# Which engine weighs which gathered rows in the attention layer of a two-layer graph network

## The chip, the cores and the metric

The kernel runs on one core of a Trainium2 chip. The core has five engines that matter here, each with its own queue of instructions that it works through strictly in order: PE (TensorE, matrix products), DVE (VectorE), ACT (ScalarE), POOL (GpSimd, which here does hardly anything but issue the gathers) and SP (SyncE, which issues the plain transfers). They meet only through semaphores. The metric is the time of one execution on the device in microseconds (us), lower is better, given as the median of several executions.

## The reference

Two graph layers work on 1250 nodes of 512 features and 40000 edges, of which each has a source and a destination. The first layer is an attention (8 heads of 64 channels) followed by a feed-forward network (FFN), the second adds edge features, sums over edges and runs two dense layers with batch norms. The change lies in the attention, where each edge's row `xl[src]` is weighted and the weighted rows of a destination are summed:

```python
xl = (x @ Wl).reshape(-1, HEADS, C)
xr = (x @ Wr).reshape(-1, HEADS, C)
h = jax.nn.leaky_relu(xl[src] + xr[dst], NEG_SLOPE)
e = jnp.einsum('ehc,hc->eh', h, att)
m = jax.ops.segment_max(e, dst, num_segments=N_NODES)
ex = jnp.exp(e - m[dst])
denom = jax.ops.segment_sum(ex, dst, num_segments=N_NODES)
alpha = ex / (denom[dst] + 1e-16)
msg = alpha[..., None] * xl[src]
out = jax.ops.segment_sum(msg, dst, num_segments=N_NODES)
```

After it come a residual sum, a layer norm and `gelu(h @ W1 + b1) @ W2 + b2`, and then the second layer.

## The kernel before

**Stages.** The profiled execution has four stretches. Up to some 99 us the kernel sorts the nodes by their number of edges, projects the nodes and writes the table `xl_t` to memory. From there to some 880 us runs the attention with its FFN mixed in. Then comes the second layer's sum over edges (to some 1330 us) and its dense end.

**Blocks, groups, chunks.** The nodes are put in ten blocks of 128, one node for each partition, by number of edges. A block of `KB[b]` edge slots (25 to 44) is cut into groups of at most 20 slots, and a group into chunks of four or five (`parts(n, CN)`; the very first chunk has two). There are 22 groups and 77 chunks, 28 chunks of five rows and 48 of four. A *row* is one slot of the chunk: 128 partitions by 512 values (8 heads by 64, with one more column for each head). A chunk's rows are gathered by POOL, one indirect transfer for each row, into a buffer `xg`, of which there are seven (`GB`).

**One step of the main loop** (in `attention`) takes chunk c of the present group and one chunk of the group before:

1. `scores(g, c)`: POOL's gathers for the chunk are queued; DVE does a max, a min, a product with signs (all into `z`) and a reduction into `S`. At a group's last chunk `softmax` follows on DVE.
2. Small pieces of other work are queued: parts of the FFN and of the norms of finished blocks.
3. `weigh` of one chunk of the group before. DVE multiplies the last rows of the chunk with their weights `w` in a single product (`V.tensor_mul`). ACT weighs the first `na` rows, each as eight instructions (one for each head, 128 partitions by 64 values, with the weight as scale). After each ACT row one part of the FFN is queued (`some(1)`), and after the rows what is left of the step's quota of three or four parts. A part is four products `pu` on PE, a GELU `uT` on ACT and a product into `py` on PE. Only then come PE's products that add the chunk's rows up (`add_up`, tile `sums`), taken from the two ends of the chunk in turn: the last row, the first, the last but one, the second and so on. The last row is always DVE's and the first always ACT's.
4. At a group's last chunk `exp(g)` is queued on ACT and gives the weights `w` of the present group.

When a group's sums are complete, `leave()` copies them with ACT (`ab`), folds them with PE (`pacc`), and `merge` adds them with DVE (`acc`). Finished blocks go through `head_of` (transposes on PE, `aT` and `hT` and a square root `rs` on ACT, sums and statistics on DVE) and then through the FFN.

**What sets the order.** `V`, `A`, `T` and `G` are wrapped so that each engine runs in the order of the program. A buffer `xg` is free for a new gather once PE has summed its rows; with seven buffers and groups of four chunks the sums of a step free the buffer of the chunk that DVE scores three steps later.

**The line that is changed** sets `na` in `weigh`. Before, it gives ACT one row of each chunk in the last group; elsewhere it gives two rows of four, and two and three rows of five in turn (two where `c` is even, three where it is odd). ACT has 166 of the 333 rows in all.

Of the kernel before, what the change touches and what calls it, by code (L numbers as in the profile page):

```python
# [725 lines left out]
def gnn_kernel(ctx, tc, x, src, dst, edge_attr, ln1_g, ln1_b, Wl, Wr, att, gat_bias,  # L726
# [519 lines left out]
    def attention(s1, xb_t, xo_t, eb_t, back, lone, follow):  # L1246
# [281 lines left out]
        def some(n):  # L1528
            for _ in range(min(n, quota[0])):
                quota[0] -= 1  # L1530
                part()
# [43 lines left out]
        def row_of(g, j):  # L1575
            c = [i for i, (c0, cn) in enumerate(g["cuts"]) if c0 <= j < c0 + cn][0]
            return g["xg"][c][:, j - g["cuts"][c][0], :].rearrange("p (h c) -> p h c", c=CX)[:, :, 1:]

        def add_up(g, j, i):

            row = row_of(g, j)
            for k in range(2):
                r = slice(k * H2, k * H2 + H2)
                T.matmul(heads(g["sums"][k][i * H2:i * H2 + H2, :]), ident[r, r], row[r], start=not g["at"][i],
                         stop=g["at"][i] == g["rows"][i] - 1)
            g["at"][i] += 1

        def weigh(g):

            w, n = g["w"], g["n"]  # L1590
            g["gd"] = gd = sp.tile([P, HEADS], F32, name="gd")
            V.tensor_reduce(gd, w[:, :n, :].rearrange("p n h -> p h n"), axis=AX.X, op=OP.add)
            g["at"], g["rows"] = [0, 0], [sum((cn + 1 - i) // 2 for _, cn in g["cuts"]) for i in range(2)]
            for c, (c0, cn) in enumerate(g["cuts"]):
                na = 1 if g is groups[-1] else (cn + c % 2) // 2
                rest = leave()
                xv = g["xg"][c][:, na:cn, :].rearrange("p n (h c) -> p n h c", c=CX)[:, :, :, 1:]
                V.tensor_mul(xv, xv, w[:, c0 + na:c0 + cn, :, None].to_broadcast([P, cn - na, HEADS, CH]))
                for j in range(c0, c0 + na):
                    xv = row_of(g, j)  # L1600
                    for h in range(HEADS):
                        A.activation(xv[:, h, :], xv[:, h, :], AF.Copy, scale=w[:, j, h:h + 1])
                    some(1)
                    next(rest, 0)
                some(quota[0])
                for _ in rest:
                    pass
                if not c:
                    g["sums"] = [aq.tile([P, D], F32, name=f"sums{k}") for k in range(2)]
                for j in range(cn):  # L1610
                    add_up(g, c0 + j // 2 if j % 2 else c0 + cn - 1 - j // 2, j % 2)
                yield
            weighed.append(g)

        def leave():

            if weighed:
                g = weighed.pop()
                g["pacc"] = pacc = aq.tile([P, D], F32, name="pacc")
                for k in range(2):  # L1620
                    ab = bp.tile([P, D], F32, name="ab")
                    A.copy(ab, g["sums"][k])
                    yield
                    T.matmul(pacc[k * H2:k * H2 + H2, :], fold, ab, start=True, stop=True)
                folded.append(g)
# [50 lines left out]
        groups, weighed, folded = [], [], []  # L1676
# [8 lines left out]
        for i, g in enumerate(groups):  # L1685
# [14 lines left out]
            for c in range(nc_):  # L1700
# [4 lines left out]
                if c == 0:  # L1705
                    if not i:
                        others.append(wr_order())
                    if g["first"] and g["b"] != ORDER[-1]:
                        others.append(slots_of(g["b"] - 1))
                    if g is groups[-1] and held["xx"] < 3:  # L1710
                        rows_of(blk)
                    weighing = weigh(groups[i - 1]) if i else None
# [24 lines left out]
        for _ in weigh(g):  # L1737
            if folded:
                merge(folded.pop())
# [278 lines left out]
```

## Time and profile before

| what | value |
|---|---|
| median of 9 runs | 1482.49 us (1477.83 to 1486.03) |
| the profiled execution's own time | 1483.55 us |
| its span in the profile | 1481.8 us |
| granted TensorE clock | 0.912 |

Busy time of each engine in the four stretches, in us:

| stretch | PE | DVE | ACT | POOL |
|---|---|---|---|---|
| 0 to 150 | 91.8 | 116.9 | 68.1 | 74.9 |
| 150 to 880 | 592.0 | 605.8 | 507.5 | 464.2 |
| 880 to 1330 | 376.5 | 357.1 | 85.1 | 313.2 |
| 1330 to 1482 | 113.9 | 65.1 | 54.6 | 13.8 |

How to read what follows. The groups of instructions give out<-in by the program's tile names, the shapes, a count, then after the bar the busy time in us and the mean duration of one in ns, then the engine's idle time just before them and what ended it. The waits give who waited for whom, the total in us, how many times, and the longest. The timeline gives the start in us, a duration in us, the engine, the line, the instruction and a count of equal ones that were merged; in square brackets stands the engine's idle time before it and what ended that. All instructions of the attention carry the line of one helper, L782, so they are told apart by their tiles. ACT's small instructions overlap: eight of them are 2.02 us from first start to last end, though each lasts some 345 ns.

### The profile page before, as it was taken

Reading aid. Unit: us, or ns where it says so; the run is one execution under the profiler, and the core shown is the slowest. Engines: PE = TensorE matmul, PEld = TensorE weight load, DVE = VectorE, ACT = ScalarE, POOL = GpSimd, SP = SyncE. Lnnn points to the kernel's source line nnn. Section 1 sums busy time; section 2 is a strip of 40 time slices with the busy share of each in tenths; the row PEclk is TensorE's granted clock in tenths of the full one; section 3 lists DMA queues with packets and bytes.
Section 4 is the critical chain, followed back from the end, with each engine's and each line's share of the span. In section 5 each row is a group of like instructions: output and inputs, shape, how many; then the busy total and the mean of one; then the engine's idle time right before and its main releaser. Section 6 shows DMA issues by size and latency. Waiting matters only on the chain. (4 is left out here: it accounts for less than half of the span.)

```text
span 1481.8 us, 16505 instructions
## 1 busy us (share of the span) xinstructions
PE 1174.3 (79%) x5204; PEld 559.8 (38%) x5204; DVE 1144.9 (77%) x1472; ACT 715.3 (48%) x2063; POOL 866.0 (58%) x789
## 2 busy tenths in 40 slices
PE   6845659898988795978797797787787999898893
PEld 4431115344534442424353363222222443334452
DVE  7859898978888979898899512798988889877133
ACT  4525476867777676777856841111111222212533
POOL 2357777755577877674774003777777777750002
PEclk9977779999999798989898998999989999999996
DMA  6246966655566657553563043877777777760001
GB/s 223 93 144 175 397 181 180 181 146 154 147 186 181 191 174 195 167 160 109 159 177 94 19 153 112 292 238 245 229 233 235 231 239 242 224 180 22 0 0 72
DMA packets 89152, 251.16 MB, mean 170 GB/s; under 512 B 17214, under 2 KB 19268, under 8 KB 88543
## 3 DMA queue, kind: packets, MB, share of 16 engines
q0 software_dynamic: 61008, 199.11, 46.0%
q1 hardware_dynamic: 28047, 50.91, 9.6%
q8 instruction: 43, 0.70, 0.2%
q14 instruction: 54, 0.44, 0.1%
HBM read 225.86 MB, written 24.22 MB: 169 GB/s over the span
## 5 line engine op out<-in xcount | busy, mean ns | idle before, releaser
L782 POOL DMA_INDIRECT xg<-xl_t,src_i x333 | 422.2, 1268 | 197.8 <-issue 117.1
L749 POOL DMA_INDIRECT xs<-xb_t,src_i x333 | 314.9, 946 | 113.2 <-issue 59.4
L782 ACT ACTIVATE xg<-xg,w 128x64 f32<-128x64 f32 x1328 | 331.0, 344 | 0.1
L782 PE MATMUL sums<-xg,ident 64*64 64x512 f32 x1332 | 212.6, 715 | 112.4 <-DVE xg L782 105.0
L1826 PE MATMUL pe<-we,eaT 64*128 64x512 f32 x666 | 206.8, 683 | 71.5 <-DVE xs L1871 67.1
L782 DVE TENSOR_TENSOR z<-xg,nxr 128x1440 f32<-128x1440 f32 (+4 forms) x154 | 197.7, 1325 | 41.9 <-DMA xg<-xl_t,src_i 41.4
L782 DVE TENSOR_REDUCE S<-z 128x32 f32<-128x2080 f32 (+2 forms) x77 | 192.2, 2496 | 2.6
L782 PEld LDWEIGHTS pu<-hT,w 128*128 128x128 f32 x1280 | 165.9, 198 | 68.7 <-issue 58.1
L1871 DVE TENSOR_TENSOR xs<-xs,pe 128x1024 f32<-128x1024 f32 (+1 forms) x130 | 153.6, 1187 | 35.2 <-DMA xs<-xb_t,src_i 29.3
L782 PE MATMUL pu<-hT,w 128*128 128x128 f32 x1280 | 174.4, 285 | 0.0
L782 PE MATMUL py<-w,uT 128*128 128x512 f32 x320 | 163.4, 602 | 12.5 <-ACT uT L782 12.3
L1872 DVE SCALAR_TENSOR_TENSOR pd<-xs,pd 128x1024 f32<-128x1024 f32 (+1 forms) x130 | 155.7, 1198 | 3.3
L782 PEld LDWEIGHTS sums<-xg,ident 64*64 64x64 f32 x1332 | 60.0, 154 | 253.5 <-DVE xg L782 126.0
L1826 PEld LDWEIGHTS pe<-we,eaT 64*128 64x128 f32 x666 | 60.0, 198 | 169.9 <-DVE xs L1871 123.0
L1868 ACT ACTIVATE xs<-pe 128x1024 f32<-128x1024 f32 x40 | 41.0, 1024 | 160.0 <-PE pe L1867 136.6
L782 DVE TENSOR_TENSOR xg<-xg,w 128x1024 f32<-128x1024 f32 (+2 forms) x77 | 100.1, 1305 | 0.0
L782 ACT ACT_TABLE_LOAD x71 | 91.1, 1283 | 7.3 <-DVE sh L782 4.3
L782 PE MATMUL pacc<-ab,fold 128*64 128x512 f32 x88 | 55.0, 711 | 42.9 <-ACT ab L782 41.6
L741 POOL DMA_INDIRECT out_dram<-z,v_i x10 | 10.0, 1002 | 130.5 <-ACT z L782 128.0
L1867 PE MATMUL pe<-xs,ident 128*128 128x512 f32 x160 | 83.0, 628 | 2.0 <-DMA xs<-xb_t,src_i 1.9
L782 DVE TENSOR_TENSOR z<-z,sgn 128x768 f32<-128x768 f32 (+2 forms) x77 | 78.2, 1015 | 0.0
L782 PE MATMUL pz<-z,v 128*128 128x512 f32 (+1 forms) x192 | 71.0, 529 | 6.2 <-ACT z L782 6.2
(264 smaller groups left out, 1286.7 us busy)
## 6 DMA issues: line engine op xcount, KB each, us to landing
eb_t<-fe SPq DMA_DIRECT2D x38, 256.0 KB
ea<-eb_t SPq DMA_DIRECT2D x38, 256.0 KB
w<-in_L_gnn_W_dram SPq DMA_DIRECT2D x8, 1024.0 KB
xg<-xl_t,src_i POOLq DMA_INDIRECT x333, 3.9
xs<-xb_t,src_i POOLq DMA_INDIRECT x333, 3.8
v<-in_L_gnn_W_dram SPq DMA_DIRECT2D x2, 2048.0 KB
xo_t<-xo SPq DMA_DIRECT2D x10, 256.0 KB
x_out<-xo_t SPq DMA_DIRECT2D x10, 256.0 KB
```

What stands on the lines that cost most here:

```text
L741: s = nc.gpsimd.indirect_dma_start(out=table, out_offset=bass.IndirectOffsetOnAxis(ap=idx, axis=0), in_=rows, in_offset=None, bounds_check ...
L749: return nc.gpsimd.indirect_dma_start(out=rows, out_offset=None, in_=table, in_offset=bass.IndirectOffsetOnAxis(ap=idx, axis=0))
L782: ins = getattr(engine, name)(*args, **kw)
L1826: nc.tensor.matmul(pe[:, k, :], eaTs[n][r, j // 2, :], we[r, :], start=True, stop=not by_pe(i))
L1867: nc.tensor.matmul(pe[:, k, :], ident, xs[:, k, :], start=False, stop=True)
L1868: nc.scalar.activation(xv, pe, AF.Relu)
L1871: add = nc.vector.tensor_add(xv, xv, pe[:, :m, :])
L1872: nc.vector.scalar_tensor_tensor(pv, xv, 0.0, pv, op0=OP.max, op1=OP.add)
```

## The change

In every group but the last, ACT now has three rows of every chunk of five, and of chunks of four two rows (where `c` is even) and three (where it is odd). DVE has the rest.

```diff
             for c, (c0, cn) in enumerate(g["cuts"]):
-                na = 1 if g is groups[-1] else (cn + c % 2) // 2
+                na = 1 if g is groups[-1] else (cn + 1 + c % 2) // 2
                 rest = leave()
                 xv = g["xg"][c][:, na:cn, :].rearrange("p n (h c) -> p n h c", c=CX)[:, :, :, 1:]
                 V.tensor_mul(xv, xv, w[:, c0 + na:c0 + cn, :, None].to_broadcast([P, cn - na, HEADS, CH]))
                 for j in range(c0, c0 + na):
                     xv = row_of(g, j)
                     for h in range(HEADS):
                         A.activation(xv[:, h, :], xv[:, h, :], AF.Copy, scale=w[:, j, h:h + 1])
                     some(1)
                     next(rest, 0)
                 some(quota[0])
```

By the cuts of the groups this moves one row from DVE to ACT in 31 of the 77 chunks: in the 12 chunks of five with an even `c`, and in the 19 chunks of four with an odd `c`. ACT's rows go from 166 to 197. In the built program DVE's product goes from 24 by 64 values in each partition to 16 by 64 in the first kind, from 16 by 64 to 8 by 64 in the second, and ACT gets eight instructions more for each. The third row's FFN part, queued by `some(1)`, comes out of the same quota, so PE's and POOL's instructions are the same in number.

## The prediction

> **What bounds the kernel now.** First the windows, cut at the stages: the change touches 99 to 850 us only. In the row for 150 to 880 us the columns are the stretch, its length, the busy time of PE, PE's weight loads, DVE, ACT and POOL, then clock, DMA share and GB/s.
>
> ```profile
> 150.00:880.00 730.00, 591.98 (x3109) 292.57 (x3110) 605.84 (x687) 507.54 (x1683) 464.19 (x370) 0.91 0.57 168
> 250.00:300.00 50.00, 42.71 (x232) 19.33 (x228) 49.25 (x53) 39.63 (x129) 35.90 (x29) 0.94 0.65 181
> ```
>
> DVE is busiest (83%), PE close behind (81%), ACT has 70%. No engine is the bound alone: three queues wait on each other in turn. So I read next, in the same stage, the groups with shapes kept apart and the waits:
>
> ```profile
> L782 ACT ACTIVATE xg<-xg,w 128x64 f32<-128x64 f32 x1247 | 311.3, 345 | 0.1
> L782 DVE TENSOR_TENSOR xg<-xg,w 128x1024 f32<-128x1024 f32 x60 | 72.5, 1214 | 0.0
> L782 DVE TENSOR_TENSOR xg<-xg,w 128x1536 f32<-128x1536 f32 x13 | 22.7, 1749 | 0.0
> DVE z L782 <- DMA xg<-xl_t,src_i: 32.0, 13, 5.9
> DVE gd L782 <- ACT w L782: 12.5, 4, 7.0
> PE sums L782 <- DVE xg L782: 82.6, 21, 6.8
> PE sums L782 <- ACT xg L782: 3.2, 5, 0.8
> ACT hT L782 <- PE pt L782: 46.3, 10, 7.1
> ```
>
> The sums wait for DVE far oftener than for ACT, which speaks for moving rows away from DVE. But DVE's own longest single wait on ACT is 7.0 us, for the weights `w`, and ACT's idle time (730 - 507.5 = 222 us) is not spread evenly: it lies in waits for PE's transposes and projections. What counts is therefore where each added row falls: in front of such a wait, or inside a run in which ACT never rests.
>
> **The change, part by part.** *Removed from DVE:* 31 rows. Three rows cost 1749 ns, two 1214, so a row is 0.535 us; for a product cut from two rows to one I take the same step (the one-row product of the first chunk lasts 0.68 us, again 0.53 less). 31 x 0.535 = 16.6 us of DVE time. *Added to ACT:* 31 x 8 instructions. In the timeline 16 of them take 3.93 us and 8 take 2.02, so eight more are 1.91 us; 31 x 1.91 = 59 us. ACT would go to (507.5 + 59) / 730 = 78%, DVE to 81%. *Moved:* the third row's FFN part. It stays ahead of the sums in PE's queue, but its GELU sits behind one more ACT row. That is 1.9 us, and the part's product into `py` comes three parts (over 5 us of PE work) later, so I cost it at nothing; without that cover it would cost PE up to 1.9 us a step. The gathers are not moved, but a buffer comes free later where the sums end later. The new row also comes before its neighbour in the sums of chunks of four (last, first, third, second), so two rows (0.9 us) follow ACT's end instead of one.
>
> Behind the added row wait, on ACT's queue: the next GELUs, the copies `ab`, the weights `w`, the root `rs`. For `w` and `rs` DVE waits, for `ab` PE. I lined up the 77 chunks from the timeline (end of DVE's product, end of ACT's rows, the sums) and followed a delay through each stretch that has affected chunks, until an idle gap takes it up:
>
> 1. *99 to 250 us: -2.1.* DVE hardly rests, ACT waits for it. Four of six affected chunks give their 0.535 us. The other two (183 to 200 us) give nothing: there the sums already end on ACT's rows.
> 2. *250 to 306 us: +1.2.* Four affected chunks, and ACT is busy 39.6 of 50 us. Two rows from 254 on push `w`, `ab` and `acc` until a 2.1 us gap at 267 takes half; the sums at 277 move by 2.0, the rows before 284 by 1.6 + 1.9, and `hT` at 288.3 by 1.2, after PE's own idle time before the sums (1.6 us) is eaten. DVE waits for this chain at 300.5 (5.2 us), so its 4 x 0.535 is lost.
> 3. *306 to 366 us: +0.8.* The row added at 323 ends after DVE's product and holds the sums by 0.8; the other two cancel (+0.3 and -0.4).
> 4. *366 to 432 us: 0.* Three affected chunks, in front of ACT waits of 0.9 to 4.7 us; DVE's gain becomes more waiting for gathers (4.3 us at 420).
> 5. *432 to 470 us: +1.9.* ACT's rows end at 441.7 and the sums at 442.8. One more row (with 0.9 us of sums behind it instead of 0.5) moves the sums, then PE's projection, the next sums, and with them the buffer that POOL waits for at 456; DVE waits for just that gather. (The stretch's second affected chunk stands before 6 us of ACT idleness.)
>
> ```profile
> 439.65 2.01 ACT L782 ACTIVATE xg<-xg,w 128x64 f32<-128x64 f32 x8
> 440.87 1.95 PE L782 MATMUL sums<-xg,ident 64*64 64x512 f32 x16
> 455.14 1.95 PE L782 MATMUL sums<-xg,ident 64*64 64x512 f32 x16
> 457.89 2.29 POOL L782 DMA_INDIRECT xg<-xl_t,src_i  x1 [1.80 <-ACT xg L782]
> 469.55 2.94 DVE L782 TENSOR_TENSOR z<-xg,nxr 128x1800 f32<-128x1800 f32 x2 [5.09 <-DMA xg<-xl_t,src_i]
> ```
>
> 6. *470 to 500 us: -1.1.* Two affected chunks with PE waiting for DVE (5.0 and 5.5 us).
> 7. *500 to 706 us: 0.* Three affected chunks, each before 1.4 to 4.7 us of ACT idleness and with the sums 5 us after ACT.
> 8. *706 to 756 us: +1.1.* ACT runs without a gap from 705.8 to 737.8 and gets three rows, +5.7. The gap of 4.8 before `hT` (742.6) takes most; `hT` comes at 737.8 + 5.7 = 743.5 or just after, some 1.1 later, and with it `rs`, for which DVE already waits 2.1 us.
> 9. *756 to 814 us: -1.6.* DVE never waits; three rows less.
> 10. *814 to 841 us: +3.8.* ACT's run from `hT` to `w` has no gap, two of its four chunks get a row, and DVE waits for `w`:
>
> ```profile
> 814.43 1.51 ACT L782 ACTIVATE hT<-pt,cols 128x128 f32<-128x128 f32 x4 [6.52 <-PE pt L782]
> 824.40 3.93 ACT L782 ACTIVATE xg<-xg,w 128x64 f32<-128x64 f32 x16
> 833.50 3.93 ACT L782 ACTIVATE xg<-xg,w 128x64 f32<-128x64 f32 x16
> 837.45 1.28 ACT L782 ACT_TABLE_LOAD   x1
> 838.74 0.26 ACT L782 ACTIVATE w<-S 128x72 f32<-128x72 f32 x1
> 839.04 0.27 DVE L782 TENSOR_REDUCE gd<-w 128x8 f32<-128x64 f32 x1 [7.01 <-ACT w L782]
> ```
>
> After it comes the tail of the attention, which the second layer waits for: DVE's product, the sums, the fold, the last block's FFN. None of it has slack, so +3.8 goes to the end.
>
> Sum of the ten: -2.1 + 1.2 + 0.8 + 1.9 - 1.1 + 1.1 - 1.6 + 3.8 = +4.0 us. The profiled execution took 1483.55 us (its span 1481.8 and 1.75 around it), so 1487.5; it is 1.1 above the median of the nine runs, and from that median I forecast 1482.5 + 4.0 = 1486.5.
>
> What the trace of before cannot show is how the queues settle after several shifts. From below: every chunk whose sums start 0.1 us after DVE's product gives its 0.535 and no wait on ACT grows. I count 14, so -7.5. From above: every affected chunk whose sums end 3 us or less after ACT's rows (ten) passes on the whole row: 10 x 1.91 = +19. I take +4.0, nearer to the first, since most rows fall before gaps.
>
> *A rule against the change.* In the rows a moved row costs ACT 1.91 us and spares DVE 0.535. The Trainium skill, "ScalarE: Activation LUTs", section "Rules for kernel authors", says that multiplications belong on VectorE and not on ScalarE. By that rule alone the sum would be 59 - 16.6, some 42 us slower; the waits above say that most of it lies in ACT's gaps, and the waits decide here.
>
> *A rule on the gathers.* In the trace a gather's issue takes 0.95 us beside DVE's reductions, and more beside its products of two tensors:
>
> ```profile
> 506.17 2.94 DVE L782 TENSOR_TENSOR z<-xg,nxr 128x1800 f32<-128x1800 f32 x2 [1.99 <-DMA xg<-xl_t,src_i]
> 506.55 2.47 POOL L782 DMA_INDIRECT xg<-xl_t,src_i  x1 [0.30 <-issue]
> 510.21 2.86 DVE L782 TENSOR_REDUCE S<-z 128x40 f32<-128x2600 f32 x1
> 511.30 0.95 POOL L782 DMA_INDIRECT xg<-xl_t,src_i  x1 [0.30 <-issue]
> ```
>
> The Trainium skill, "SBUF — State Buffer", section "Who interferes with whom", infers that a product of two tensors does not stall descriptor generation. By the page shorter products give POOL nothing; by the rows POOL gains up to 0.5 us in a chunk. I put it at nothing: only eight affected chunks lie where DVE waits for gathers (390 to 690 us), 8 x 0.535 = 4.3 us at most, which the lower end covers.
>
> **The rivals.**
>
> - *DVE leads after all (faster).* For it: PE's sums wait 82.6 us for DVE and 3.2 for ACT. Against it: the run from 814 to 841 us, where DVE itself waits for ACT. It needs ACT's backlog to clear before `w` and `rs`; it decides from the point where the losses of points 2, 3, 5, 8 and 10 (8.8 us together) stay under the gains. With the 14 direct chunks: 1482.5 - 7.5 = 1475.
> - *ACT becomes the bound (much slower).* For it: with four rows more the window 250 to 300 has 39.6 + 7.6 = 47 busy us of 50. Against it: most affected chunks are followed by 1.4 to 7 us of idle ACT. Ten whole rows: 1482.5 + 19 = 1501.5.
> - *It cancels.* Gains of points 1, 6, 9 (-4.8) against the tail (+3.8) alone: 1481.5, no change that can be told.
>
> That the change doesn't do what it says can be left out: the built program has the shorter products and the added instructions.
>
> **How the numbers follow.** My sum 0.52, cancelling 0.16, DVE leads 0.20, ACT bound 0.12. The likeliest is the sum: 1486.5, with a range of its own of 1482 to 1493. To leave out no more than two in ten, the range reaches down into the first rival and up into the second: 1476 to 1497. A measurement of this kernel can tell some 0.2% (3 us) from no change. Faster by more: 0.20 and a little of the cancelling case, 0.22. Within: the rest of that case and the low edge of the sum, 0.20. Slower by more: 0.58.
>
> **What would show it.** Right: DVE's products 16.6 us shorter in total, ACT's weighing 59 longer; DVE's wait for `w` near the end of the attention up from 7.0 to 11 or 12 us (3.8, and the 1.1 that its products lose just before); waits of the sums on ACT up, on DVE down; the second layer as long as before. Wrong: DVE's idle time unchanged and the attention ending earlier, or sums waiting on ACT in most affected chunks.

## The result

The changed kernel takes 1489.89 us (median of 10 runs, 1485.57 to 1492.39), the kernel before in the same comparison 1480.83 us (31 runs): ratio 1.0061, 95% interval 1.0047 to 1.0074, so 9.0 us slower (7.0 to 11.0). The profiled execution took 1490.06 us, its span 1488.3 us; before it was 1483.55 and 1481.8 us. The forecast was 4.0 us slower: the sign and the range hold, the size was too small by 5.

The groups of the page after, ACT's weighing, DVE's products with the weights, and the gathers' issue on POOL (count, then busy us and mean ns):

```profile
L782 POOL DMA_INDIRECT xg<-xl_t,src_i x333 | 409.1, 1229 | 208.3 <-issue 110.2
L782 ACT ACTIVATE xg<-xg,w 128x64 f32<-128x64 f32 x1576 | 392.0, 345 | 0.1
L782 DVE TENSOR_TENSOR xg<-xg,w 128x512 f32<-128x512 f32 (+2 forms) x77 | 83.6, 1090 | 0.0
```

ACT's weighing is 61 us longer (331.0 before), DVE's products 16.5 us shorter (100.1), the gathers' issue 13 us shorter (422.2). The waits of the attention after, from 150 to 885 us (total us, times, longest):

```profile
PE sums L782 <- DVE xg L782: 56.7, 17, 6.5
PE sums L782 <- ACT xg L782: 22.0, 17, 2.7
DVE z L782 <- DMA xg<-xl_t,src_i: 35.8, 13, 5.8
DVE rs L782 <- ACT rs L782: 17.3, 8, 6.6
DVE gd L782 <- ACT w L782: 15.1, 3, 9.4
```

PE waits 26 us less for DVE and 19 us more for ACT; DVE waits for ACT's `rs` 17.3 us (10.7 before), and its longest wait for `w` is 9.4 us (7.0). The end of the attention on ACT and DVE, as a timeline:

```profile
835.26 5.85 ACT L782 ACTIVATE xg<-xg,w 128x64 f32<-128x64 f32 x24
841.13 1.28 ACT L782 ACT_TABLE_LOAD   x1
842.42 0.26 ACT L782 ACTIVATE w<-S 128x72 f32<-128x72 f32 x1
```

```profile
842.72 0.27 DVE L782 TENSOR_REDUCE gd<-w 128x8 f32<-128x64 f32 x1 [9.45 <-ACT w L782]
```

The last chunk's run on ACT is 24 instructions now, and `w` comes at 842.42 instead of 838.74. In this execution the stage before the attention happened to end 3.1 us earlier than in the profile of before, so shifts on the path are read against that: here `w` is 3.7 + 3.1 = 6.8 us late. Read so, in the stretches of the prediction:

| stretch, us | forecast | trace |
|---|---|---|
| 99 to 250 | -2.1 | -1.3 |
| 250 to 306 | +1.2 | +0.9 |
| 306 to 366 | +0.8 | +2.4 |
| 366 to 432 | 0 | +0.5 |
| 432 to 470 | +1.9 | +2.2 |
| 470 to 500 | -1.1 | -0.7 |
| 500 to 706 | 0 | -0.9 |
| 706 to 756 | +1.1 | +2.5 |
| 756 to 814 | -1.6 | -2.6 |
| 814 to 841 | +3.8 | +3.8 |
| 841 to 850 | 0 | +1.7 |
| after | 0 | +1.1 |
| sum | +4.0 | +9.6 |

Each number is the difference between the shift of one instruction (the end of a chunk's sums, or the start of a product of DVE) at the end of the stretch and at its start; it is one pair of executions, good to about 1 us. Most entries have the forecast sign; three are larger by 1.4 to 1.7 us. One part is not a matter of ACT's or DVE's time at all. PE around 420 us, before and then after:

```profile
419.65 3.59 PE L782 MATMUL sums<-xg,ident 64*64 64x512 f32 x16 [2.61 <-DVE xg L782]
...
424.91 3.84 PE L782 MATMUL pu<-hT,w 128*128 128x128 f32 x32
```

```profile
417.44 1.19 PE L782 MATMUL sums<-xg,ident 64*64 64x512 f32 x8 [1.97 <-DVE xg L782]
420.70 1.99 PE L782 MATMUL sums<-xg,ident 64*64 64x512 f32 x8 [2.07 <-ACT xg L782]
...
423.66 2.07 PE L782 MATMUL py<-b,one 1*128 1x512 f32 x2
425.66 5.92 PE L782 MATMUL pu<-hT,w 128*128 128x128 f32 x32
```

The sums start 2.2 us earlier in the record, but stop in the middle for 2.07 us, for ACT's third row. Then the same 32 products `pu` take 5.92 us instead of 3.84. The windows give the reason (stretch, length, then busy time of PE, PE's weight loads, DVE, ACT and POOL; then the granted clock). Before, and then after:

```profile
420.00:425.00 5.00, 5.00 (x23) 1.82 (x15) 0.70 (x2) 1.35 (x5) 3.78 (x5) 0.66 0.62 172
425.00:430.00 5.00, 4.16 (x33) 3.85 (x34) 4.97 (x4) 5.00 (x21) 3.10 (x4) 1.00 0.83 233
```

```profile
418.00:423.00 5.00, 2.93 (x18) 0.69 (x11) 0.68 (x1) 2.65 (x12) 3.72 (x5) 0.68 0.70 195
423.00:428.00 5.00, 5.00 (x17) 3.17 (x16) 4.97 (x5) 4.23 (x16) 2.84 (x4) 0.50 0.83 226
```

The granted clock falls to half in both, but stays there for 3.4 us (420.0 to 423.4) before and for 10.2 us (419.8 to 430.0) after. The same happens at the end, from 843 us: 3.4 us before, 10.2 after. There the last sums show it, before and then after:

```profile
845.23 4.56 PE L782 MATMUL sums<-xg,ident 64*64 64x512 f32 x32
```

```profile
845.25 1.97 PE L782 MATMUL pacc<-ab,fold 128*64 128x512 f32 x2 [3.00 <-ACT ab L782]
847.90 1.97 PE L782 MATMUL pacc<-ab,fold 128*64 128x512 f32 x2 [0.68 <-ACT ab L782]
849.79 5.38 PE L782 MATMUL sums<-xg,ident 64*64 64x512 f32 x32
```

### The profile page after: what moved, and what is told of

Same layout as the page of the kernel before. It is cut to its first block, busy times and chain, and to the rows that moved or that the text cites. A ratio compares the mean times of both kernels' runs of the same rounds, so it can differ in the third digit from the quotient of the medians.

```text
span 1488.3 us, 16761 instructions
## 1 busy us (share of the span) xinstructions
PE 1185.1 (80%) x5204; PEld 557.4 (37%) x5204; DVE 1128.8 (76%) x1472; ACT 772.7 (52%) x2311; POOL 849.6 (57%) x789
## 5 line engine op out<-in xcount | busy, mean ns | idle before, releaser
L782 POOL DMA_INDIRECT xg<-xl_t,src_i x333 | 409.1, 1229 | 208.3 <-issue 110.2
L782 ACT ACTIVATE xg<-xg,w 128x64 f32<-128x64 f32 x1576 | 392.0, 345 | 0.1
L782 PE MATMUL sums<-xg,ident 64*64 64x512 f32 x1332 | 218.7, 717 | 105.9 <-DVE xg L782 78.9
L782 PE MATMUL py<-w,uT 128*128 128x512 f32 x320 | 163.2, 601 | 14.4 <-ACT uT L782 14.3
L782 PEld LDWEIGHTS sums<-xg,ident 64*64 64x64 f32 x1332 | 56.6, 156 | 260.1 <-DVE xg L782 98.0
L1867 PE MATMUL pe<-xs,ident 128*128 128x512 f32 x160 | 86.1, 649 | 2.1 <-DMA xs<-xb_t,src_i 2.1
L782 DVE TENSOR_TENSOR xg<-xg,w 128x512 f32<-128x512 f32 (+2 forms) x77 | 83.6, 1090 | 0.0
```

The source lines that it names most:

```text
L782: ins = getattr(engine, name)(*args, **kw)
L1867: nc.tensor.matmul(pe[:, k, :], ident, xs[:, k, :], start=False, stop=True)
```

## The experiments

Each run was timed against the kernel before on the same chip; 1% is 14.8 us. Where a difference to the changed kernel is named, it is the difference of two ratios, and with both intervals it is good to some 3 us either way.

**The two halves alone.** `dve_half` gives DVE the shorter products and leaves ACT's rows, so 31 rows are not weighted at all; `act_half` adds ACT's instructions (its first row a second time, with a scale `unit` of one) and leaves DVE's products.

```diff
 dve_half, against the changed kernel
-                na = 1 if g is groups[-1] else (cn + 1 + c % 2) // 2
+                na = 1 if g is groups[-1] else (cn + c % 2) // 2
+                nd = 1 if g is groups[-1] else (cn + 1 + c % 2) // 2
...
-                V.tensor_mul(xv, xv, w[:, c0 + na:c0 + cn, :, None].to_broadcast([P, cn - na, HEADS, CH]))
+                V.tensor_mul(xv, xv, w[:, c0 + nd:c0 + cn, :, None].to_broadcast([P, cn - nd, HEADS, CH]))
 act_half, against the kernel before
+                extra = g is not groups[-1] and (cn + 1 + c % 2) // 2 > na
...
+                    if extra and j == c0 + na - 1:
+                        x0 = row_of(g, c0)
+                        for h in range(HEADS):
+                            A.activation(x0[:, h, :], x0[:, h, :], AF.Copy, scale=unit)
+                        some(1)
+                        next(rest, 0)
```

> DVE's half of the change alone: its products are as short as in the changed kernel, ACT weighs what it weighed before, so in 31 chunks one row goes into the sums unweighted (that part of the computation is left out). Theory (the gain is real but only where PE waits for DVE): 14 direct chunks at 0.535 us, 5 to 8 us faster than before, ratio 0.9945 to 0.9970. Rival 1 (DVE leads everywhere): 16.6 us faster, 0.989. Rival 2 (DVE's products are hidden): no change, within 2 us.

> ACT's half of the change alone: DVE's products as before, and in the 31 chunks ACT runs eight more instructions of the same shape (it multiplies its first row a second time, by one) ahead of its last row. Theory (the change is the sum of a gain on DVE and a larger loss on ACT): the change's 9 us and the 5 to 8 us that DVE's half no longer gives back, 13 to 17 us slower than before, ratio 1.009 to 1.0115. Rival (ACT's gaps take the rows up, and the change's loss is something else): 0 to 4 us slower.

Measured: `dve_half` 0.9903 (0.9882 to 0.9925), 14.4 us faster; `act_half` 1.0101 (1.0081 to 1.0121), 15.0 us slower. The first misses its expectation and nearly meets the rival: of the 16.6 us taken from DVE some 14 come out at the end, where the prediction had counted on 4.8 us that reach it. The waits of `dve_half`:

```profile
PE sums L782 <- DVE xg L782: 68.0, 21, 6.9
DVE z L782 <- DMA xg<-xl_t,src_i: 35.6, 16, 5.9
PE sums L782 <- ACT xg L782: 3.0, 4, 0.8
```

PE waits 14.6 us less for DVE than before and no more for ACT, and DVE's wait for gathers grows by only 3.6 us. DVE's gain is thus not swallowed by the gathers, since earlier sums also free the buffers earlier. The second is as expected. But -14.4 and +15.0 make +0.6, and the change is +9.0: some 8 us, by the three intervals good to 5 either way, belong to neither half. What the change has and neither half has is that the sums wait for a row that DVE no longer weighs. In `act_half` the last row that ACT works on is also the last of ACT's to be summed, in chunks of four the last of all, and in its trace the clock has no half stretch at 420 us.

**Which chunks.** `five_only` and `four_only` make the change in one kind of chunk. By the cuts there are 27 chunks of five rows and 49 of four, not 28 and 48.

```diff
 five_only, against the kernel before
-                na = 1 if g is groups[-1] else (cn + c % 2) // 2
+                na = 1 if g is groups[-1] else (cn + (cn == 5) + c % 2) // 2
 four_only, against the kernel before
+                na = 1 if g is groups[-1] else (cn + (cn == 4) + c % 2) // 2
```

> The change in the 12 chunks of five rows alone (three rows for ACT where it was two); the chunks of four as before. Theory (what costs are the chunks of four, where after ACT's row two rows of sums follow instead of one, and which stand in the ACT runs at 420, 442 and 833 us): the chunks of five stand mostly where DVE leads: 5 of them give 0.535 us, those at 229 to 260 us lose some 1 to 2 us: between 3 us faster and no change, ratio 0.998 to 1.000, and the 19 chunks of four carry all of the 9 us. Rival (the cost is spread evenly over the moved rows): 12/31 of 9 us, 3.5 us slower, 1.0024.

> The change in the 19 chunks of four rows alone (three rows for ACT where it was two, odd c); the chunks of five as before. Theory (the parts add up): the change was 9.0 us slower, the chunks of five alone 1.3 us faster (0.9991), so the chunks of four alone cost 9 to 11 us, ratio 1.006 to 1.0075. Rival (the loss is an interaction, in which the rows of the chunks of five make ACT late for those of four): 2 to 5 us slower only, 1.0015 to 1.0035.

Measured: `five_only` 0.9991 (0.9973 to 1.0009), `four_only` 1.0072 (1.0054 to 1.0089). The parts add up: -1.3 and +10.7 make +9.4. The rival of an even price (1.0024) lies outside the first interval. All of the loss comes from the chunks of four. Those are the ones in which ACT's third row is not the last to be summed, but they also stand elsewhere in the program (both chunks of the tail are of four), and these two runs do not part the order from the place. The next one does.

**The order of the sums.**

```diff
 order, against the changed kernel
+                turn = [c0 + j // 2 if j % 2 else c0 + cn - 1 - j // 2 for j in range(cn)]
+                if cn == 4 and na == 3:
+                    turn[2:] = turn[:1:-1]
                 for j in range(cn):
-                    add_up(g, c0 + j // 2 if j % 2 else c0 + cn - 1 - j // 2, j % 2)
+                    add_up(g, turn[j], j % 2)
```

> The change, with another order of the sums in chunks of four where ACT has three rows: last, first, second, third instead of last, first, third, second, so that one row of sums (0.5 us) follows ACT's third row and not two (1.0 us). In the trace of the change the sums end within 2.1 us of ACT's last row in ten such chunks. Theory (part of the loss is this second row behind ACT's end, and the longer pause of PE in front of it): 0.5 us in some six of the ten, and the half-clock stretch at 420 us shorter: 2 to 5 us faster than the change, ratio to before 1.0025 to 1.0045. Rival (what waits behind ACT's row is w and rs on ACT's own queue, not the sums): as the change, 1.0055 to 1.0065.

Measured: 1.0036 (1.0022 to 1.0051), 3.7 us faster than the change, as the theory had it; the rival's 1.0055 lies outside. PE at the same place:

```profile
413.63 1.79 PE L782 MATMUL sums<-xg,ident 64*64 64x512 f32 x8 [0.70 <-DVE xg L782]
416.25 1.07 PE L782 MATMUL sums<-xg,ident 64*64 64x512 f32 x4 [0.83 <-ACT xg L782]
418.16 1.08 PE L782 MATMUL sums<-xg,ident 64*64 64x512 f32 x4 [0.83 <-ACT xg L782]
...
420.80 3.84 PE L782 MATMUL pu<-hT,w 128*128 128x128 f32 x32
```

One wait of 2.07 us has become two of 0.83 with a row of sums between them, and the `pu` behind them run at full clock again. PE's waits for ACT's rows fall from 22.0 to 16.2 us in all. The place at 420 us is not the whole of it: in this pair of traces the sums of `order` are 2.5 us ahead before it, 5.9 behind it and 7.8 at the end of the attention, and the profiled execution is the lowest of its eight.

**The clock.** `warm` keeps the change and lets PE add products with zero weights to the sums while it waits for the third row in four chunks.

```diff
 warm, against the changed kernel
+    WARM = {(9, 1), (9, 3), (20, 1), (20, 3)}
...
+        def nothing(g, j, k):
+
+            row, r = row_of(g, j), slice(k * H2, k * H2 + H2)
+            T.matmul(heads(g["sums"][k][0:H2, :]), zeros[r], row[r], start=False, stop=False)
...
                 for j in range(cn):
+                    if j == 2 and (gi, c) in WARM:
+                        for k in range(4):
+                            nothing(g, c0 + cn - 1, k % 2)
                     add_up(g, c0 + j // 2 if j % 2 else c0 + cn - 1 - j // 2, j % 2)
```

> The kernel with the change, with four products of zero weights (each as long as one product of the sums, added on to them) on PE in front of the third row of four chunks: (9,1), (9,3), (20,1), (20,3), where PE waits 0.3 to 3 us for ACT's added row and where the granted clock then fell to half for some 10 us in the trace of the change, against 3.4 us before. Theory (the wait empties PE and the clock is lowered for longer): without the pause the two long half-clock stretches at 420 and 843 us go back to some 3.4 us, 3 to 5 us faster than the change, ratio to before 1.003 to 1.004. Rival (the half-clock stretches come by other causes, the added products only cost their time, about 0.5 us in each chunk): as the change or up to 2 us slower, 1.006 to 1.0075.

Measured: 1.0030 (1.0014 to 1.0045), 4.6 us faster than the change, within the theory's range and clear of the rival's 1.006. The kernel does strictly more work on PE than the change and is faster. Its trace at 418 and 845 us:

```profile
418.11 1.88 PE L782 MATMUL sums<-xg,zeros 64*64 64x512 f32 x8
421.22 1.09 PE L782 MATMUL sums<-xg,ident 64*64 64x512 f32 x8 [1.23 <-ACT xg L782]
...
423.88 3.84 PE L782 MATMUL pu<-hT,w 128*128 128x128 f32 x32
```

```profile
418.00:423.00 5.00, 3.77 (x27) 1.22 (x20) 2.08 (x2) 3.23 (x15) 3.75 (x3) 1.00 0.68 186
423.00:428.00 5.00, 4.72 (x34) 3.77 (x34) 4.93 (x6) 5.00 (x20) 3.78 (x5) 1.00 0.72 201
...
846.00:850.00 4.00, 3.88 (x32) 1.20 (x24) 3.26 (x8) 0.06 (x1) 0.00 (x0) 0.88 0.00 0
```

ACT's row comes no earlier than in the change (its run ends at 421.2 us, there at 420.7), but the clock stays at 1.00 at 420 us, and the stretch at 843 is 3.4 us long again. The gain arises at these two places: the sums of `warm` are 0.6 us behind those of the change at 417 us and 2.8 ahead at 434, and 2.8 ahead at 828 and 5.4 at 848. Over all executions the granted clock averages 0.914 in `warm`, 0.907 with the change and 0.911 before. So the pause costs time through the clock, 4.6 us of the 9, good to 3 either way. The gains of `order` and `warm` overlap (both remove the half-clock stretch at 420 us), so they are not to be added.

Not every such pause has this price. At 740 us, where `warm` adds nothing, PE has the same waits of 0.72 and 2.74 us for ACT's rows as in the change, first in the change and then in `warm`:

```profile
742.00 1.98 PE L782 MATMUL sums<-xg,ident 64*64 64x512 f32 x8 [2.74 <-ACT xg L782]
746.96 3.78 PE L782 MATMUL pu<-hT,w 128*128 128x128 f32 x16
```

```profile
739.41 1.09 PE L782 MATMUL sums<-xg,ident 64*64 64x512 f32 x8 [2.74 <-ACT xg L782]
742.07 2.05 PE L782 MATMUL pu<-hT,w 128*128 128x128 f32 x16
```

The clock is at half for 10.2 us there in the one (from 740.7) and not at all in the other. A stretch of half clock in one trace is therefore partly chance; the times and clocks over all executions carry the result.

**The tail.** `tail_undone` takes the rows of the last large group (20) out of the change; `relief_tail` takes one row of ACT in each of that group's four chunks out of the kernel before.

```diff
 tail_undone, against the changed kernel
-                na = 1 if g is groups[-1] else (cn + 1 + c % 2) // 2
+                na = 1 if g is groups[-1] else (cn + (g is not groups[-2]) + c % 2) // 2
 relief_tail, against the kernel before
+    LESS = {(20, 0),(20, 1),(20, 2),(20, 3)}
...
-                na = 1 if g is groups[-1] else (cn + c % 2) // 2
+                gi = [o is g for o in groups].index(True)
+                na = 1 if g is groups[-1] else (cn + c % 2) // 2 - ((gi, c) in LESS)
```

> The changed kernel without its two added rows in the last group but one (the run of ACT that ends with the weights DVE waits for). Theory (the end of the attention carries 3.7 us of the loss and 1.8 us more from PE's slower clock behind it): 5.5 us faster than the changed kernel, 3.5 us slower than before, ratio 1.0024. Rival (the loss is spread evenly over the 31 rows, 0.29 us each): 0.6 us faster than the changed kernel, ratio 1.0057.

> The kernel before, with ACT one row less (and DVE one row more) in each of the four chunks of group 20, weighed between 817 and 838 us. Theory (ACT's run from hT to the weights w has no gap and sets the end of the attention there): w comes 4 x 1.91 = 7.6 us earlier; DVE's products in front of gd get 4 x 0.535 = 2.1 us longer, so DVE (done with its last product at 832.0) is ready at 834.1 instead of 839.0: 4.9 us faster than before, ratio 0.9967; DVE's wait for w falls from 7.0 us to under 1. Rival 1 (PE's sums, not w, set that stretch): no change, ratio 0.999 to 1.001, the wait moves to sums or xo. Rival 2 (DVE leads): 2.1 us slower, 1.0014.

Measured: `tail_undone` 1.0031 (1.0017 to 1.0045), with the theory's 1.0024 inside and the rival's 1.0057 outside, so two rows of 31 carry 4.4 us of the 9.0. `relief_tail` 0.9980 (0.9967 to 0.9993), 3.0 us faster than before, less than the 4.9 expected. Its trace contradicts the mechanism: ACT's queue now waits where it used to weigh.

```profile
831.64 0.37 ACT L782 ACTIVATE uT<-pu,cols 128x128 f32<-128x128 f32 x1 [3.17 <-PE pu L782]
833.39 0.37 ACT L782 ACTIVATE uT<-pu,cols 128x128 f32<-128x128 f32 x1 [1.38 <-PE pu L782]
...
836.98 0.26 ACT L782 ACTIVATE w<-S 128x72 f32<-128x72 f32 x1
```

From `hT` (812.82 here, 814.43 before) to `w` it is 24.2 us, 24.3 before, though ACT has four rows less, and DVE's wait for `w` is 5.34 us instead of the expected 1 or less. PE's products `pu`, which stand behind 32 products of sums, are late next. ACT was the longest chain there by almost nothing: in the traces added rows cost fully, and removed rows give nothing at `w`. What the 3 us come from instead is open; one trace with a shift of 0.7 us at the end of the attention does not show it.

**Choosing chunks by who is late.** `lead_only` adds a row to ACT only where ACT ended 2 us or more ahead of DVE's product (15 chunks, the set `MORE` below without `LESS`), `both` also takes one from ACT in 14 chunks where ACT was late.

```diff
 both, against the kernel before
+    MORE = {(1, 2),(3, 0),(3, 2),(7, 3),(8, 3),(10, 3),(11, 1),(12, 3),(14, 3),(16, 3),(17, 0),(17, 2),(19, 1),(19, 2),(19, 3)}
+    LESS = {(4, 1),(5, 1),(6, 1),(6, 2),(7, 0),(7, 2),(9, 3),(11, 3),(13, 3),(15, 3),(20, 0),(20, 1),(20, 2),(20, 3)}
...
+                na = 1 if g is groups[-1] else (cn + c % 2) // 2 + ((gi, c) in MORE) - ((gi, c) in LESS)
```

> The kernel before, with one row more for ACT in 15 chunks only, chosen in the trace of before as those where ACT's rows end 2 us or more before DVE's product does. Theory (a moved row costs only where ACT has no gap): 4 to 8 us faster than before (15 x 0.535 = 8.0 at most), ratio 0.9945 to 0.9973. Rival (each moved row costs 0.29 us wherever it is): 4.4 us slower, 1.003.

> The kernel before with ACT one row more in the 15 chunks where ACT ended two or more us ahead of DVE's product (the run lead_only), and one row less in 14 chunks where ACT's run is in front of w, rs or ab and the sums end on ACT's rows (k = 13, 16, 19, 20, 21, 23, 32, 40, 48, 56 and the four of group 20). The rows of ACT are 167, as before 166. Theory (where a row stands counts, not how many each engine has): the 3.1 us of lead_only, 4.9 us of the tail, and 0 to 3 us of the other ten together: 8 to 11 us faster than before, ratio 0.9926 to 0.9946. Rival (DVE is the bound, so that 14 rows given back to it cost 7.5 us against 8.0 gained): 0.998 to 1.001.

Measured: `lead_only` 0.9979 (0.9964 to 0.9993), 3.1 us faster, a little less than expected; `both` 0.9953 (0.9934 to 0.9972), 7.0 us faster, with the theory's range just missed and the rival's (0.998 to 1.001) outside the interval. With 167 rows on ACT instead of 166, but differently placed, the kernel is faster.

**The clock behind DVE's waits.** `both_warm` fills eight of PE's waits for DVE with products of zero weights.

```diff
 both_warm, against both
+    WARM = {(5, 2): 4, (10, 3): 7, (12, 3): 9, (13, 1): 9, (14, 3): 4, (15, 1): 4, (19, 2): 6, (19, 3): 6}
...
+        def nothing(g):
+
+            for k in range(2):
+                r = slice(k * H2, k * H2 + H2)
+                for q in range(0, 2 * P, P):
+                    T.matmul(g["sums"][k][0:H2, q:q + P], zeros[r], ident[r], start=False, stop=False)
...
+                for _ in range(WARM.get((gi, c), 0)):
+                    nothing(g)
                 for j in range(cn):
```

> The kernel of the run both (ACT one row more in 15 chunks, one less in 14), with products of zero weights added on to the sums while PE waits for DVE in front of eight chunks: (5,2), (10,3), (12,3), (13,1), (14,3), (15,1), (19,2), (19,3), where PE waited 2.9 to 6.0 us and the clock then was at half for 3.4 to 14 us. 4 to 9 times about 0.5 us each, meant to end before DVE does. Theory (the lowered clock after PE's waits costs time there too): the half-clock time between 150 and 885 us falls from 126 us to 80 or less, and the time by 3 to 8 us against both, ratio to before 0.990 to 0.9935. Rival (behind these waits DVE leads and PE has slack again, so that the clock falls where it costs nothing): the half-clock time falls, the time stays, 0.9945 to 0.9965.

Measured: 0.9912 (0.9890 to 0.9933), by the ratio 13 us faster than before (the medians are 1466.85 and 1481.15 us) and 6 us faster than `both`, good to 4 either way. This beats both kernels. One of the eight places, in `both` and then in `both_warm`:

```profile
557.73 4.59 PE L782 MATMUL sums<-xg,ident 64*64 64x512 f32 x20 [5.80 <-DVE xg L782]
```

```profile
547.15 4.20 PE L782 MATMUL sums<-ident,zeros 64*64 64x128 f32 x72
552.36 2.79 PE L782 MATMUL sums<-xg,ident 64*64 64x512 f32 x20 [1.01 <-DVE xg L782]
```

The products of zeros fill most of the wait for DVE, and the 20 products of sums behind it take 2.79 us instead of 4.59. The half-clock stretches that begin between 150 and 885 us add up to 85 us instead of 126, the granted clock averages 0.926 over the executions instead of 0.915, and in this pair of traces the attention ends 7.4 us earlier than in `both`. The lead goes up and down: 3.4 us at the sums after (5,2), 5.7 at 434 us (where nothing was added), 9.5 at 490, 3.1 at 648, 7.4 at the end.

**Where DVE leads.** `early_warm` does the same in four more chunks between 150 and 220 us.

```diff
 early_warm, against both_warm
-    WARM = {(5, 2): 4, (10, 3): 7, (12, 3): 9, (13, 1): 9, (14, 3): 4, (15, 1): 4, (19, 2): 6, (19, 3): 6}
+    WARM = {(1, 2): 9, (2, 2): 7, (3, 1): 10, (3, 2): 6, (5, 2): 4, (10, 3): 7, (12, 3): 9, (13, 1): 9, (14, 3): 4, (15, 1): 4, (19, 2): 6, (19, 3): 6}
```

> The kernel of the run both_warm (0.9912) with products of zero weights in front of four more chunks, (1,2), (2,2), (3,1) and (3,2), weighed from 150 to 220 us, where PE waited 4.1 to 6.2 us for DVE and the clock was at half for 37 us of 70. Theory (a lowered clock costs only where some later wait for PE is on the path): between 150 and 250 us DVE rests 5.9 us at 174 (for the sums folded there) and 5.5 us at 235 (for pacc) and else not at all, so only what reaches these two waits counts: half-clock time between 150 and 885 us from 85 to 60 us or less, time by 1 to 4 us against both_warm, ratio to before 0.9885 to 0.9905. Rival (DVE leads there, PE's time is hidden): the half-clock time falls, the time stays or gets worse by the added products, 0.991 to 0.993.

Inconclusive. In this comparison the kernel before itself took 1604.20 us (17 runs) and this one 1608.58, ratio 1.0011 (0.9973 to 1.0049). The largest difference to the other traces is the second layer, with PE busy 323 of 450 us between 880 and 1330 us instead of 369 or more. The whole comparison ran 8% slower, before included, so its ratio cannot be set beside the other eleven. Against the theory's other number, the half-clock time is 89 us and did not fall to 60; whether filling these four waits pays stays open. But this kernel holds everything that `both_warm` has, and 0.9912 lies outside its interval: either the gain of `both_warm` does not hold on this slower chip, or the four added places cost it. The granted clock was raised here too (0.887 against 0.872), so a higher clock alone did not make the kernel faster. `both_warm` was not run there.

## Why the prediction was right, and where it was short

- *The two engines' work* was right: -16.5 us against 16.6, +61 against 59.
- *The tail, 814 to 841 us* (+3.8) was right in place and size: `w` comes 3.7 us later in the record. DVE's wait for it rose from 7.0 to 9.45 us instead of 11 to 12, since 2.45 us more of DVE's rest now lie just before, in its wait for `xo` (2.96 us, before 0.51), which stands behind the same ACT rows; together 11.9. `tail_undone` confirms it: 4.4 us with the tail's clock included.
- *"None of it has slack, so +3.8 goes to the end"* was right, but stopped there. PE's pause for the added row moved the clock as well, and the last folds and sums took another 1.7 us. More generally the sum has no term for PE's clock. `warm` puts the price of the pauses in four chunks at 4.6 us (good to 3 either way), about as much as the forecast was short by.
- *366 to 470 us* (0 and +1.9) was short by 0.8 us in that table, and by more at its peak, +5.5 at 465 us, part of which DVE's gain in the next stretches takes back. The step that failed here is point 4: chunk (9,1)'s added row was costed at nothing, because ACT's rest of 0.9 to 4.7 us stood behind it. What it delays, the sums on PE, was not behind that rest. Behind it went a 10.2 us stretch at half clock.
- *306 to 366 and 706 to 756 us* were short by 1.6 and 1.4 us. In the first the trace after has a half-clock stretch of 3.4 us (at 351.5) that before has not; in the second PE waits 2.7 us for ACT's rows at 739 us, followed by 10.2 us at half clock, which the same wait in `warm` was not. No run took these apart.
- *The sums' order.* The prediction named the 0.9 us of sums behind ACT's end and used it only in point 5. `order` shows that, with the clock, it was worth 3.7 us over the whole (good to 3 either way).
- *DVE's gain.* Points 2, 4 and 7 let it vanish behind waits for ACT or for gathers. `dve_half` shows 14.4 us if ACT is not late. The runs give a larger gain (14.4) against a larger loss (15.0, and some 8 that neither half shows alone). The forecast had both sides too small, and that its net came nearer than its parts is luck.
- *The gathers.* Their issue fell by 13 us of POOL time, put at nothing. In `dve_half` it fell by only 4.8 us (422.2 to 417.4), and the change lost in spite of it, so it decided nothing.
- *The rule against the change*, that products belong on DVE, would have given 42 us. The row moved costs 1.91 us on ACT and spares 0.535 us on DVE, and yet 15 such rows in the right chunks make the kernel 3.1 us faster. In this case place decides, not the ratio of the durations.

## What to carry to other kernels

Before moving work to an engine with idle time, look not only at the rest behind each added piece but at who else waits for the piece itself, and in which order the consumer takes its inputs: the late input belongs last. Then choose the places one by one, from the ends of the two engines in the trace, instead of by a formula over all of them. And where PE pauses for a few us ahead of work that something waits for, compare the granted clock behind the pause: filling the pause with products of zero weights can be worth as much as shortening it (4.6 against 3.7 us here, each good to 3).

## What the runs showed of the hardware

Half-clock stretches in the attention come in multiples of 3.4 us (3.4, 6.8, 10.2, 13.7) and start at waits as short as 2 to 3 us: behind 2.61 us before (3.4 us long), in the second of two waits of 1.97 and 2.07 us with 1.19 us of work between them in the change (10.2 us long, though PE shows no further rest from 420.70 to the end of that stretch). Within one trace all of them begin on one grid of 3.41 us: in the trace of before the stretches at 420.0, 478.0 and 843.3 us are 17 and 107 such steps apart. From trace to trace the grid stands elsewhere, which fits the two outcomes of the same wait at 740 us; that the grid is their cause was not tested. The Trainium skill, "TensorE: Matmul & The Clock Gate", section "HAM oscillation — how this bites in real kernels", gives as its rule no idle gaps of PE above some 3.4 us. The page's 3.4 us agrees with the length of the stretches, but shorter gaps were enough here, and the measurement decides.

With products of zeros in PE's waits the granted clock stayed at 1.00 (418 to 428 us in `warm`, 546 to 566 us in `both_warm`, where `both` has 0.66 in the matching 10 us).

A gather's issue on POOL takes 0.946 us on average where no operation of two tensors on DVE overlaps it by more than 0.03 us (88 of 333 before, 95 after) and 1.383 us where one does (245 before; 1.341 after, 238). The Trainium skill, "SBUF — State Buffer", section "Who interferes with whom", infers that descriptor generation is not stalled by such an operation. The rows speak against it, though no run here was made for that alone.
